# Thirteen whole quads of a graph kernel's key/value gather loaded row by row, in place of one tile of each of 42 quads

## The chip, the cores and the metric

The kernel runs on one core of one Trainium2 chip. The metric is device time in microseconds (us), from the launch of the one program to its end; lower is better. Each kernel is timed in several runs, and the median is shown with the lowest and the highest. The profile is one further execution, recorded by the hardware profiler; its span goes from the first to the last recorded instruction.

## The reference

A graph layer with attention-like edge weights, a residual and a layer norm. There are 6250 nodes with 128 features and 206250 edges, sorted by receiving node (`dst`); `src` are the senders.

```python
w_ij  = silu(edge_feats @ rad_W1 + rad_b1) @ rad_W2 + rad_b2
w_ij += silu(chi_scalar @ sph_W1 + sph_b1) @ sph_W2 + sph_b2          # per edge, 128
q_i   = (node_feats @ Wq)[receivers]
k_j   = (node_feats @ Wk)[senders]
v_j   = (node_feats @ Wv)[senders]
alpha = (q_i * w_ij * k_j).sum(over the 16 of each of 8 heads) / sqrt(16) * cutoffs
out   = segment_sum(alpha * v_j, receivers) / 16
x     = layernorm(x + out)                                            # rows without scale or shift
```

## The kernel before

**Tiling.** Edges lie on the 128 partitions. A tile is 128 edges, a quad four tiles (`QT = 4`, 512 edges), a group four quads (`NQ = 4`). There are 403 quads (`QUADS`) in 101 groups (`NG`). A prologue computes K and V of all nodes (`k_and_v`), writes them to a table in DRAM, `kv_tab`, with 1 KB a node (`ROW_BYTES`), and prepares index tables. For the first ten quads (`XQ`) K and V are computed from gathered rows of x; for the 393 others they are gathered from `kv_tab`.

**The gather.** `gathers(q)` lets POOL (GpSimd) issue one indirect DMA a tile (L132, through the helper `gather`): it fetches the 1 KB rows of 128 senders into one quarter of a `kv` buffer. There are `RING = 16` such buffers, and the gather of the quad 14 positions ahead (`AHEAD`) is issued in each slot of the main loop, with a wait on the matmuls of an earlier quad.

**The main loop** (L746 to L808) has one slot a quad, in the order 0, 2, 1, 3 within a group (the list `order`). In a slot, each engine's queue gets its work in the order of the code:

- PE: sums of messages of the group before (L616), the two first layers of the quad two ahead (`first_layers`, L518, into two `ph` buffers), q at the edges of the next quad (L527), the second layers of the next quad (`weigh`, L560 and L565). One slot in a group also has the sum over a whole group (L657, L659).
- ACT (ScalarE): the two silus of the quad two ahead (L548; the first waits for the q matmuls of L527), between them two row loads (`next_rows(2)`), then a copy out of PSUM, and at the end of the slot up to four more row loads (`rows_at_end`). Once in 16 slots `statistics` normalizes four groups: a table load for the square root, L682, four L696, and a table load back before the next silu.
- DVE (VectorE): `multiply` (L577, q times K; it reads `kv`), `scores` (L585, L587, L591), `messages` (L604, alpha times V), and one-hot matrices (`hotT` L264 from `relb`, `hot` L269).
- SP: the DMA queue for x rows (L283), edge features (L224), `relb` (L235), the result's rows (`write_rows`, L708), and row loads (L191).

**Rows loaded singly.** 42 quads of the 403 (`ROW_TILES`, positions `row_at`) have only three of their four tiles gathered by POOL. The fourth is loaded by 128 single DMAs of 1 KB, whose addresses come from registers: `load_rows(i)`, called at the end of slot i, has SP load 32 addresses into registers (L186, `ROW_UNIT`) and issue 32 DMAs (L191), two and a half times a tile (80 rows); and ACT loads 24 addresses (`ROW_UNIT_ACT`) and issues 24 DMAs, twice a tile (48 rows, `ROW_ACT`), spread over slots by `next_rows` and `rows_at_end`. The rows of a tile go out over the 8 or 9 slots between two such quads and are complete 8 slots (`ROW_LEAD`) before use. They land in a `wide` buffer, of which there are three, and `multiply` waits for their count on a semaphore (`row_sems`). As the tiles of such a quad lie in two buffers (`kv_parts`), L577 and L604 run twice there, over 384 and 128 columns.

**The result's rows.** `normalize` puts four results into the list `written`; `write_rows`, one call a slot, pops one and queues its DMA on SP. The call stands ahead of `statistics` in the slot, so the first row of a batch is queued in the slot after its normalization.

Of the kernel before, what the change touches and what calls it, by code (L numbers as in the profile page):

```python
# [65 lines left out]
def gnn_kernel(ctx, tc, x, src, dst, weight, edges, rad_W1, rad_b1, rad_W2, rad_b2,  # L66
# [77 lines left out]
    row_sems = [tc.alloc_semaphore(f"rows_{n}") for n in range(ROW_SEMS)]  # L144
    row_count = [0] * ROW_SEMS

    def next_rows(n):
# [16 lines left out]
    def gathers(q, marks=()):  # L164

        kv = quad_of("kv", RING, 2 * D)
        for t in range(QT - 1 if q in row_quads else QT):
            o = gather(kv[:, t, :], kv_tab, src_i[:, q * QT + t:q * QT + t + 1])
            if marks:
                tc.add_manual_dep(o.ins, marks[t].ins.name, WAIT, reason="no gather ahead of TensorE")  # L170
        kv_of[q] = kv

    def load_rows(i):

        k = next((k for k in range(ROW_TILES) if i <= row_at[k] - ROW_LEAD), None)
        start = len(order) if k is None else (row_at[k - 1] if k else ROW_FIRST) - ROW_LEAD + 1
        if i < start:
            return rows_at_end() if k is None else None
        q = order[row_at[k]]
        n = P - ROW_ACT  # L180
        slots, units = row_at[k] - ROW_LEAD + 1 - start, math.ceil(n / ROW_UNIT)
        a, b = ((j * units + slots - 1) // slots for j in (i - start, i - start + 1))
        table = kv_tab.bitcast(U8).rearrange("(o n) b -> o (n b)", o=1)

        def registers(e, m, engine):
            return nc.values_load_multi_w_load_instructions(  # L186
                at_i[k:k + 1, e:e + m], engines=(engine,), min_val=0,
                max_val=(N - 1) * ROW_BYTES, skip_runtime_bounds_check_because="senders are nodes")[1]

        def one_row(engine, p, r):  # L190
            return engine.dma_start(row_of[q][p:p + 1, 0, :].bitcast(U8), table[:, ds(r, ROW_BYTES)])  # L191

        def rows_of_act(first, m):
            rows = registers(first, m, ACT)
            for p in range(m):
                yield lambda p=p: signalled(one_row(nc.scalar, first + p, rows[p]))

        def signalled(o):
            tc.no_tile_sem_insts.add(o.ins.name)
            tc.add_to_no_dep_group(f"rows_{q}", o.ins)  # L200
            o.then_inc(row_sems[k % ROW_SEMS], 16)
            row_count[k % ROW_SEMS] += 16
            row_done[q] = row_sems[k % ROW_SEMS], row_count[k % ROW_SEMS]
# [12 lines left out]
    def kv_parts(q, t):  # L216

        if q not in row_quads:
            return [(t, kv_of[q][:, t, :])]
        return [(slice(0, QT - 1), kv_of[q][:, :QT - 1, :]), (slice(QT - 1, QT), row_of[q])]  # L220

# [85 lines left out]
    with tc.tile_pool(name="nodes", bufs=1) as nodes, \  # L307
# [79 lines left out]
        def row_bytes():  # L387
            for k, i in enumerate(row_at):
                c = order[i] * QT + QT - 1
                nc.vector.tensor_scalar(rows_f[:, k:k + 1], src_i[:, c:c + 1],  # L390
                                        float(ROW_BYTES), None, op0=OP.mult)
# [120 lines left out]
    with tc.tile_pool(name="ps", bufs=1, space=PSUM) as pp:  # L512
# [57 lines left out]
        def multiply(q, mark=None, t=slice(0, QT)):  # L570
            if t.start == 0:
                kq_of[q] = quad_of("kq", 3)
            if t.start == 0 and q in row_done:
                o = nc.vector.wait_ge(*row_done[q])
                tc.declare_fence(o.ins, group=f"rows_{q}")
            for u, kv in kv_parts(q, t):
                o = nc.vector.tensor_tensor(kq_of[q][:, u, :], pq_of[q][:, u, :], kv[:, :, :D],  # L577
                                            op=OP.mult)
                if mark is not None:
                    after(o, mark)  # L580

# [16 lines left out]
        def messages(q, alpha, t=slice(0, QT), marks=()):  # L598

            if t.start == 0:  # L600
                msg_of[q] = quad_of("msg", XQ)
            for u, kv in kv_parts(q, t):
                n = u.stop - u.start
                o = nc.vector.tensor_tensor(  # L604
                    msg_of[q][:, u, :].rearrange("p t (h e) -> p t h e", e=HD),
                    kv[:, :, D:].rearrange("p t (h e) -> p t h e", e=HD),
                    alpha[:, u.start - t.start:u.stop - t.start, :, None].to_broadcast(
                        [P, n, HEADS, HD]), op=OP.mult)
                behind(o, marks, 3)

        def sum_quads(g, t, j=None):
# [6 lines left out]
            return o  # L618

        def wide_one_hots(q):  # L620

# [3 lines left out]
            nc.vector.tensor_scalar(d, d, gb[:, q // NQ:q // NQ + 1], None, op0=OP.subtract)  # L625
            hot_of[q, "wide"] = quad_of("wide", 3, P)
            nc.vector.tensor_tensor(hot_of[q, "wide"], d[:, :, None].to_broadcast([P, QT, P]),
# [116 lines left out]
        marks = weigh(order[0])  # L744
        mark = marks[-1]
        for g in range(NG - 1):  # L746
            for slot, j in enumerate((0, 2, 1, 3)):
# [34 lines left out]
                if slot == 1:  # L782
# [82 lines left out]
    def general_group(g):  # L865
        with tc.tile_pool(name="lg", bufs=1) as lg, tc.tile_pool(name="lb", bufs=1) as lb, \
# [12 lines left out]
            for j in range(NQ):  # L879
                kv = lb.tile([P, QT, 2 * D], F32, name="kv_l")  # L880
                qe = lb.tile([P, QT, D], F32, name="qe_l")
                xe = lb.tile([P, QT, D], F32, name="xe_l")
# [8 lines left out]
                for t in range(QT):  # L891
                    nc.tensor.matmul(pq[:, t, :], xe[:, t, :], wq, start=True, stop=True)
                nc.vector.tensor_copy(qe, pq)
                r0, c0 = 2 * R * (j // 2), EQ * (j % 2)
# [120 lines left out]
```

## Time and profile before

| | |
|---|---|
| median of 3 runs | 1985.04 us (1985.03 to 1985.54) |
| the profiled execution, its own time | 1985.41 us |
| its span | 1983.3 us |
| mean granted TensorE clock | 0.916 |
| ACT busy / share of the span | 752.2 us / 38% |
| DVE busy / share | 1471.1 us / 74% |
| POOL busy / share | 1488.6 us / 75% |

The busy time of an engine counts its computing instructions (and on POOL the indirect DMAs); loads of registers, semaphore waits and the issue of a DMA on SP or ACT don't count, and are listed under "SPq" and "ACTq". In a list of groups, each row has the line of the code, the engine, the operation, what it writes and reads, how often, the busy time in us and the mean in ns, and then the idle time of the engine just ahead of these instructions with what ended it. In the list of waits, a row is the engine and line that waited, what released it, the total in us, the number of times and the longest. A timeline row is start, length, engine, line and operation, and in brackets the engine's idle time before it with its releaser.

### The profile page before, as it was taken

The numbers are of one execution on the slowest core, as the hardware profiler recorded it, in microseconds if no ns is written. First come the engines' busy times: TensorE is split into PE (matmuls) and PEld (weight loads), VectorE is DVE, ScalarE is ACT, GpSimd is POOL, SyncE is SP. The second block draws the span as 40 slices with busy tenths as digits, with TensorE's granted clock in tenths as the row PEclk, the third lists the DMA queues.
The fourth block names the chain that finished last, engine by engine and source line by source line (L and its number), as shares of the span: only waits on it lengthen the run. The fifth ranks groups of instructions, "written<-read, shape, count | busy, mean of one in ns | idle before, by whom it ended". The sixth has DMA issues, their size and how long they took to land.

```text
span 1983.3 us, 55295 instructions
## 1 busy us (share of the span) xinstructions
PE 1782.5 (90%) x16014; PEld 1505.7 (76%) x16014; DVE 1471.1 (74%) x3123; ACT 752.2 (38%) x1437; POOL 1488.6 (75%) x1580
## 2 busy tenths in 40 slices
PE   9899999978997988998898888899989988898897
PEld 7788788767876877876787777777767777777786
DVE  6687777768876877776777777767767767777777
ACT  3244344333343343342343333333433433433334
POOL 7777777777777777777777777777777777777775
PEclk9899899978998998998999889989989999898988
DMA  8545545455455555454554555545545455445543
GB/s 316 160 141 156 157 145 156 142 157 156 143 157 154 146 156 154 144 160 139 159 158 140 159 142 155 158 143 154 154 145 158 144 152 159 142 142 158 157 140 90
DMA packets 150194, 304.77 MB, mean 154 GB/s; under 512 B 38732, under 2 KB 83900, under 8 KB 149884
## 3 DMA queue, kind: packets, MB, share of 16 engines
q0 software_dynamic: 74720, 203.26, 36.7%
q1 hardware_dynamic: 69632, 95.45, 14.8%
q10 hardware_dynamic: 5532, 2.47, 0.5%
q8 instruction: 128, 2.10, 0.4%
q14 instruction: 182, 1.49, 0.3%
HBM read 287.58 MB, written 13.46 MB: 152 GB/s over the span
## 4 chain that ended last, share of the span: by engine, by line
PE 56%; DMA 17%; DVE 11%; issue 6%; POOL 3%; ACTq 2%; SPq 2%; ACT 2%; DVEq 0%; POOLq 0%
PE pw L565 28%; DMA kv<-kv_tab,src_i 14%; PE pq L527 10%; PE ph L518 7%; PE po L616 4%; DVE kq L577 4%; DMA relb<-rel_lin 3%; PE pw L560 3%; ACTq L191 2%; POOL msg L132 2%; DVE side L587 2%; DVE kq L585 2%; SPq L191 1%; PE pq L657 1%; POOL kv L132 1%
## 5 line engine op out<-in xcount | busy, mean ns | idle before, releaser
L132 POOL DMA_INDIRECT kv<-kv_tab,src_i x1530 | 1447.9, 946 | 466.6 <-PE pw L565 174.2
L548 ACT ACTIVATE act<-ph,b 128x512 f32<-128x512 f32 x806 | 546.5, 687 | 1091.0 <-PE pq L527 1003.5
L565 PEld LDWEIGHTS pw<-w,act 128*128 128x128 f32 x6448 | 822.8, 207 | 105.6 <-issue 94.7
L565 PE MATMUL pw<-w,act 128*128 128x128 f32 x6448 | 902.7, 298 | 0.0
L527 PE MATMUL pq<-q,hotT 32*128 32x128 f32 x3224 | 502.9, 299 | 50.8 <-DVE hotT L264 40.4
L518 PE MATMUL ph<-feats,w 32*128 32x512 f32 x1612 | 501.2, 680 | 31.5 <-ACT act L548 30.6
L527 PEld LDWEIGHTS pq<-q,hotT 32*128 32x128 f32 x3224 | 422.8, 200 | 75.9 <-issue 55.4
L577 DVE TENSOR_TENSOR kq<-pq,kv 128x512 f32<-128x512 f32 (+1 forms) x403 | 271.8, 674 | 243.8 <-PE pq L527 121.2
L587 DVE TENSOR_REDUCE side<-kq 128x32 f32<-128x512 f32 x403 | 280.1, 695 | 43.2 <-DVE kq L585 1.4
L604 DVE TENSOR_TENSOR msg<-kv,side 128x512 f32<-128x512 f32 (+1 forms) x404 | 271.9, 673 | 42.7 <-DVE side L591 1.2
L585 DVE TENSOR_TENSOR kq<-pw,kq 128x512 f32<-128x512 f32 x403 | 274.7, 682 | 0.0
L518 PEld LDWEIGHTS ph<-feats,w 32*128 32x128 f32 x1612 | 137.9, 193 | 113.7 <-issue 58.2
L560 PE MATMUL pw<-brow,onesb 3*128 3x512 bf16 x403 | 161.9, 402 | 9.4 <-DVE kq L585 9.3
L616 PE MATMUL po<-msg,hot 128*32 128x128 f32 x3200 | 154.6, 290 | 0.0
L264 DVE TENSOR_TENSOR hotT<-relb,side 128x512 f32<-128x512 bf16 x101 | 69.0, 683 | 97.5 <-DMA relb<-rel_lin 97.4
L657 PE MATMUL pq<-part,to 128*128 128x128 f32 x200 | 45.9, 313 | 82.6 <-DVE kq L577 58.0
L591 DVE TENSOR_TENSOR side<-side,scale 128x32 f32<-128x32 f32 x400 | 80.0, 200 | 42.3 <-DVE side L587 0.5
L657 PEld LDWEIGHTS pq<-part,to 128*128 128x128 f32 x200 | 31.3, 197 | 93.0 <-issue 54.0
L616 PEld LDWEIGHTS po<-msg,hot 128*32 128x32 f32 x3200 | 71.3, 111 | 38.3 <-issue 4.8
L269 DVE TENSOR_TENSOR hot<-rel,side 128x512 f32<-128x512 f32 x100 | 66.1, 661 | 0.0
L258 PE MATMUL pq<-wq,xT 128*128 128x128 f32 x200 | 42.9, 299 | 11.2 <-DVE kq L577 11.1
L132 POOL DMA_INDIRECT msg<-in_x,src_x x40 | 38.9, 972 | 13.3 <-issue 11.6
(117 smaller groups left out, 855.6 us busy)
## 6 DMA issues: line engine op xcount, KB each, us to landing
wide<-kv_tab SPq DMA_DIRECT2D x3360, 1.0 KB
feats<-in_edges SPq DMA_DIRECT2D x101, 512.0 KB
wide<-kv_tab ACTq DMA_DIRECT2D x2016, 1.0 KB
kv<-kv_tab,src_i POOLq DMA_INDIRECT x1530
relb<-rel_lin SPq DMA_DIRECT2D x101, 128.0 KB
x<-in_x SPq DMA_DIRECT2D x101, 64.0 KB
out<-y SPq DMA_DIRECT2D x101, 64.0 KB
kv_tab<-kv SPq DMA_DIRECT2D x12, 512.0 KB
```

What stands on the lines that cost most here:

```text
L132: return nc.gpsimd.indirect_dma_start(out=o, out_offset=None, in_=table, in_offset=bass.IndirectOffsetOnAxis(ap=index, axis=0))
L518: return nc.tensor.matmul(act_of[q, i], w1[r0:r0 + R, :], feats_of[g][r0:r0 + R, c0:c0 + EQ], start=True, stop=True)
L527: o = nc.tensor.matmul(pq_of[q][:, t, :], hotT_of[g][b, t * P:(t + 1) * P], q_of[g][b, :], start=True, stop=True)
L548: o = nc.scalar.activation(act, act_of[q, i], AF.Silu, bias=b1[:, i:i + 1])
L560: nc.tensor.matmul(pw, onesb, brow.rearrange("p t d -> p (t d)"), start=True, stop=False)
L565: o = nc.tensor.matmul(pw[:, t, :], act_of[q, i][:, t * P:(t + 1) * P], w2[:, i, :], start=False, stop=(t == QT - 1 and i == 1))
L577: o = nc.vector.tensor_tensor(kq_of[q][:, u, :], pq_of[q][:, u, :], kv[:, :, :D], op=OP.mult)
L585: nc.vector.tensor_tensor(m, pw_of[q][:, t, :], m, op=OP.mult)
L587: o = nc.vector.tensor_reduce(alpha, m.rearrange("p t (h e) -> p t h e", e=HD), AX.X, OP.add)
L604: o = nc.vector.tensor_tensor(msg_of[q][:, u, :].rearrange("p t (h e) -> p t h e", e=HD), kv[:, :, D:].rearrange("p t (h e) -> p t h e", e ...
L616: o = nc.tensor.matmul(po_of[g][j * W:(j + 1) * W, :], hot_of[g][:, j * QT + t, :], msg_of[g * NQ + j][:, t, :], start=(t == 0), stop=(t = ...
L657: nc.tensor.matmul(ph[:, :D], to[:n, 0, :], part[:n, :], start=True, stop=(g == 0))
```

## The change

13 quads (`ROW_QUADS`) get all their four tiles by single rows, 52 tiles in all, and POOL gathers nothing for them (`gathers` returns at once, and such a quad takes no `kv` buffer). Of the 128 rows of a tile SP loads 64 and ACT 64, each in two units of 32 registers. `row_slots` gives each of the 52 tiles 7 or 8 slots of its own; within these ACT's rows go out against a goal for each slot, with no upper limit per slot. The four tiles of a quad lie in one new `rows` buffer (two of them, 4 KB a partition each; the three `wide` buffers of 2 KB go, and the three wide one-hots of the end are put into `rows` buffers), so `multiply` and `messages` run once over 512 columns for every quad. `write_rows` is called with 0 in a slot unless rows had been left in `written` at the end of the slot's writing before, so a batch's first row is queued two slots after its normalization; from group NG - 2 on it is called with 1 as before. In the branch for general inputs, which isn't run here, one buffer is shared.

```diff
-ROW_TILES = 42
+ROW_QUADS = 13
+ROW_TILES = ROW_QUADS * QT
-ROW_ACT = 48
-ROW_UNIT_ACT = 24
-ROW_SLOT_ACT = 6
+ROW_ACT = 64
+ROW_UNIT_ACT = 32
...
-    row_at = [ROW_FIRST + (n + 1) * (ROW_LAST - ROW_FIRST) // ROW_TILES for n in range(ROW_TILES)]
+    row_at = [ROW_FIRST + (n + 1) * (ROW_LAST - ROW_FIRST) // ROW_QUADS for n in range(ROW_QUADS)]
+    row_slots = []
+    for n, last in enumerate(row_at):
+        first = (row_at[n - 1] if n else ROW_FIRST) - ROW_LEAD + 1
+        row_slots += [first + t * (last - ROW_LEAD + 1 - first) // QT for t in range(QT)]
+    row_slots.append(row_at[-1] - ROW_LEAD + 1)
...
     def next_rows(n):
         for _ in range(min(n, len(act_now))):
             act_now.pop(0)()
-
-    def rows_at_end():
-        n = ROW_SLOT_ACT - 2
-        m = min(n, len(act_now))
-        next_rows(m)
-        if not act_now and act_rows:
-            f, e, r = act_rows.pop(0)
-            act_now.extend(f(e, r))
-            next_rows(n - m - 1)
+            act_sent[0] += 1
+
+    def rows_at_end(goal):
+        while act_sent[0] < goal:
+            if not act_now:
+                f, e, r = act_rows.pop(0)
+                act_now.extend(f(e, r))
+            next_rows(min(len(act_now), goal - act_sent[0]))
...
     def gathers(q, marks=()):
+        if q in row_quads:
+            return
         kv = quad_of("kv", RING, 2 * D)
-        for t in range(QT - 1 if q in row_quads else QT):
+        for t in range(QT):
...
-        q = order[row_at[k]]
-        n = P - ROW_ACT
-        slots, units = row_at[k] - ROW_LEAD + 1 - start, math.ceil(n / ROW_UNIT)
+        start, slots = row_slots[k], row_slots[k + 1] - row_slots[k]
+        at, t = divmod(k, QT)
+        q, n = order[row_at[at]], P - ROW_ACT
+        units = math.ceil(n / ROW_UNIT)
...
-        if i == start:
-            row_of[q] = quad_of("wide", 3, P)[:, :2, :].rearrange("p t d -> p (t d)")[:, None, :]
+        if i == start and t == 0:
+            row_of[q] = quad_of("rows", 2, 2 * D)
...
-        rows_at_end()
+        rows_at_end(k * ROW_ACT + ROW_ACT * (i - start + 1) // slots)
...
-            for u, kv in kv_parts(q, t):
-                o = nc.vector.tensor_tensor(kq_of[q][:, u, :], pq_of[q][:, u, :], kv[:, :, :D],
-                                            op=OP.mult)
+            kv = (row_of if q in row_quads else kv_of)[q]
+            o = nc.vector.tensor_tensor(kq_of[q][:, t, :], pq_of[q][:, t, :], kv[:, t, :D], op=OP.mult)
...
+        made_before = 0
         for g in range(NG - 1):
...
-                write_rows()
+                write_rows(1 if made_before or g >= NG - 2 else 0)
+                made_before = len(written)
```

`messages` is changed as `multiply` is, and `row_bytes`, in the prologue, makes the 52 columns of byte addresses by 13 instructions of four columns, where it made 42 columns by 42 instructions.

More of the change, by code (lines that the diff above doesn't have):

```diff
@@ L173, in load_rows @@
     def load_rows(i):
[L175 to L178, printed above, removed]
-        q = order[row_at[k]]
-        n = P - ROW_ACT
-        slots, units = row_at[k] - ROW_LEAD + 1 - start, math.ceil(n / ROW_UNIT)
+        k = next((k for k in range(ROW_TILES) if i < row_slots[k + 1]), None)
+        if k is None or i < row_slots[k]:
+            return
+        start, slots = row_slots[k], row_slots[k + 1] - row_slots[k]
+        at, t = divmod(k, QT)
+        q, n = order[row_at[at]], P - ROW_ACT
+        units = math.ceil(n / ROW_UNIT)
         a, b = ((j * units + slots - 1) // slots for j in (i - start, i - start + 1))
@@ L387, in row_bytes @@
         def row_bytes():
-            for k, i in enumerate(row_at):
-                c = order[i] * QT + QT - 1
-                nc.vector.tensor_scalar(rows_f[:, k:k + 1], src_i[:, c:c + 1],
+            for n, i in enumerate(row_at):
+                c = order[i] * QT
+                nc.vector.tensor_scalar(rows_f[:, n * QT:(n + 1) * QT], src_i[:, c:c + QT],
                                         float(ROW_BYTES), None, op0=OP.mult)
@@ L575, in multiply @@
                 tc.declare_fence(o.ins, group=f"rows_{q}")
[L576 to L580 removed]
+            kv = (row_of if q in row_quads else kv_of)[q]
+            o = nc.vector.tensor_tensor(kq_of[q][:, t, :], pq_of[q][:, t, :], kv[:, t, :D], op=OP.mult)
+            if mark is not None:
+                after(o, mark)
         def scores(q, t=slice(0, QT), marks=(), weighted=True):
@@ L601, in messages @@
                 msg_of[q] = quad_of("msg", XQ)
[L602 to L609, printed above, removed]
+            kv = (row_of if q in row_quads else kv_of)[q]
+            o = nc.vector.tensor_tensor(
+                msg_of[q][:, t, :].rearrange("p t (h e) -> p t h e", e=HD),
+                kv[:, t, D:].rearrange("p t (h e) -> p t h e", e=HD),
+                alpha[:, :, :, None].to_broadcast([P, t.stop - t.start, HEADS, HD]), op=OP.mult)
+            behind(o, marks, 3)
         def sum_quads(g, t, j=None):
@@ L625, in wide_one_hots @@
             nc.vector.tensor_scalar(d, d, gb[:, q // NQ:q // NQ + 1], None, op0=OP.subtract)
-            hot_of[q, "wide"] = quad_of("wide", 3, P)
+            if q != order[-2]:
+                wides.append(quad_of("rows", 2, 2 * D))
+            hot_of[q, "wide"] = wides[-1][:, :, P:] if q == order[-2] else wides[-1][:, :, :P]
             nc.vector.tensor_tensor(hot_of[q, "wide"], d[:, :, None].to_broadcast([P, QT, P]),
```

16 lines of the change are left out of this document (7 added, 9 removed).

## The prediction, made before the changed kernel ran

> **What bounds the kernel now.** I read the page first: the busy list, the chain that ended last, and the costliest group.
>
> ```profile
> PE 1782.5 (90%) x16014; PEld 1505.7 (76%) x16014; DVE 1471.1 (74%) x3123; ACT 752.2 (38%) x1437; POOL 1488.6 (75%) x1580
> ...
> PE 56%; DMA 17%; DVE 11%; issue 6%; POOL 3%; ACTq 2%; SPq 2%; ACT 2%; DVEq 0%; POOLq 0%
> ...
> L132 POOL DMA_INDIRECT kv<-kv_tab,src_i x1530 | 1447.9, 946 | 466.6 <-PE pw L565 174.2
> ```
>
> PE looks like the bound, at 90% and 56% of the chain, and POOL, at 75%, does not. But POOL's row deserves a second look: 1447.9 busy and 466.6 idle ahead of its 1530 gathers make 1914.5 us, 1.251 us a gather. The list of POOL's waits and its first and last gathers in the timeline say what the idle time is.
>
> ```profile
> POOL kv L132 <- PE pw L565: 174.2, 571, 0.3
> POOL kv L132 <- issue: 172.3, 565, 0.3
> POOL kv L132 <- DMA kv<-kv_tab,src_i: 46.0, 151, 0.3
> ```
>
> ```profile
> 54.12 1.03 POOL L132 DMA_INDIRECT kv<-kv_tab,src_i  x1 [0.30 <-DVE b_all L379]
> ...
> 1967.39 0.94 POOL L132 DMA_INDIRECT kv<-kv_tab,src_i  x1 [0.30 <-issue]
> ```
>
> No gap is longer than 0.3 us, whatever is named as its releaser. From 54.12 to 1967.39 the 1530 gathers start every (1967.39 - 54.12) / 1529 = 1.251 us: POOL is full from end to end, and the 0.3 us belong to each gather. Whether the others wait for it, VectorE's waits for gathered rows tell: first those between 520 and 860 us, then those between 900 and 1960 us, and last its waits for `relb` over the whole span.
>
> ```profile
> DVE kq L577 <- DMA kv<-kv_tab,src_i: 1.1, 1, 1.1
> ...
> DVE kq L577 <- DMA kv<-kv_tab,src_i: 83.9, 55, 3.7
> ...
> DVE hotT L264 <- DMA relb<-rel_lin: 97.4, 26, 12.3
> ```
>
> So there are two phases. In the first PE and VectorE, which start behind the gathers, catch up and hardly wait for rows. In the second they have caught up, wait for gathers 55 times, and the pace is POOL's. The end is POOL's last gather plus 1983.3 - 1967.4 = 15.9 us of tail, and the compute side has about 84 us in hand.
>
> **The change, part by part.** *Gathers.* 393 quads of four tiles less 42 leave 1530; less 52 they leave 1520. Ten gathers at 1.251 us are 12.5 us off POOL's stretch. Leaving out four in a row instead of one lets POOL run one quad ahead; the ring holds 14, so nothing else changes, and the last such position is 392 in both kernels, ahead of the tail. All four gathers of a row quad are spared there at once, so the 12.5 us are complete eleven quads before the end.
>
> *Row loads on ACT and SP.* Their prices, from the rows of the two lines (min/median/max in ns):
>
> ```profile
> L191 SPq DMA_DIRECT2D wide<-kv_tab x3360: 224/228/436, 125.0 to 1883.9; - x198
> L191 ACTq MOVE wide<-kv_tab x2016: 29/29/29, 128.9 to 1888.8; - x184
> L191 ACTq DMA_DIRECT2D wide<-kv_tab x2016: 227/228/706, 129.0 to 1888.8; - x184
> ...
> L186 SPq TENSOR_LOAD <-at_i x126: 979/1924/2497, 122.9 to 1877.2; - x126
> L186 ACTq TENSOR_LOAD <-at_i x84: 1662/1780/2070, 127.0 to 1871.1; - x84
> ```
>
> SP issues 3328 rows instead of 3360 and loads registers 104 times (32 each) instead of 126 (84 of 32, 42 of 16, the short ones near the minimum of 0.98): some 32 x 0.32 = 10 us and 42 x 0.98 - 20 x 1.92 = 3 us less over the run. SP's queue is as full as before.
>
> ACT issues 3328 rows instead of 2016, and loads 32 registers 104 times instead of 24 registers 84 times. That is 3328 / 372 = 8.9 rows a slot against 5.4. What covers them is the wait of the first silu for PE. A slot of ACT now, and PE's next first layer:
>
> ```profile
> 1003.22 0.69 ACT L548 ACTIVATE act<-ph,b 128x512 f32<-128x512 f32 x1 [2.93 <-PE pw L565]
> 1003.30 0.55 ACTq L191 DMA_DIRECT2D wide<-kv_tab  x2
> 1003.95 0.69 ACT L548 ACTIVATE act<-ph,b 128x512 f32<-128x512 f32 x1
> 1004.05 0.68 ACTq L191 DMA_DIRECT2D wide<-kv_tab  x2
> 1004.53 0.27 ACT L661 ACTIVATE tot<-pq 128x128 f32<-128x128 f32 x1
> 1004.82 0.58 ACTq L191 DMA_DIRECT2D wide<-kv_tab  x2
> 1006.60 0.69 ACT L548 ACTIVATE act<-ph,b 128x512 f32<-128x512 f32 x1 [1.80 <-PE pq L527]
> ```
>
> ```profile
> 1005.30 0.70 PE L518 MATMUL ph<-feats,w 32*128 32x512 f32 x2
> ```
>
> Two rows take 0.55 us, the second 0.32 after the first, and they lie beside the activations. Six rows end 2.18 us after the first silu's start; the next silu comes 3.38 after it. Nine rows end at 3.15: still covered, in a slot as short as this. With a register load it is another matter:
>
> ```profile
> 1031.17 0.69 ACT L548 ACTIVATE act<-ph,b 128x512 f32<-128x512 f32 x1 [2.03 <-PE pq L527]
> ...
> 1031.99 0.58 ACTq L191 DMA_DIRECT2D wide<-kv_tab  x2
> 1032.48 0.27 ACT L652 ACTIVATE part<-po 128x128 f32<-128x128 f32 x1
> 1034.57 0.47 ACTq L191 DMA_DIRECT2D wide<-kv_tab  x1
> 1035.14 0.69 ACT L548 ACTIVATE act<-ph,b 128x512 f32<-128x512 f32 x1 [2.40 <-PE pw L565]
> ```
>
> Between 1032.57 and 1034.57 ACT's queue loads 24 registers, and five rows end 3.87 us after the silu. With 32 registers (1.92 by SP's row, 1780 / 24 x 32 = 2.37 by ACT's) and nine rows (four more, 1.28) that is 5.3 to 5.7 us. The next silu is then about 2.2 late behind a slot of 3.4 us, 0.8 behind an average one (1983 / 403 = 4.9). PE forgives part: the second silu ended at 1004.64, 0.66 before PE began the next first layer, whose first half needs the first silu alone, 0.7 earlier; some 1.35 in all. So a load slot costs PE between nothing (average slot) and about 0.9 us (short slot); 104 of them cost 0 to 94 us. I take half, 47, as the recorded slots are of both kinds. What is queued behind the late silu on ACT is the copy out of PSUM and the slot's rows; who waits is PE.
>
> The slots with a table change have no such cover:
>
> ```profile
> 1015.49 1.25 ACT L696 ACTIVATE y<-y,shift,rs 128x128 f32<-128x128 f32 x3
> 1017.37 0.79 ACTq L191 DMA_DIRECT2D wide<-kv_tab  x2
> 1018.24 1.28 ACT L548 ACT_TABLE_LOAD   x1 [1.51 <-issue]
> ...
> L548 ACT ACT_TABLE_LOAD x25 | 32.1, 1283 | 7.9 <-issue 7.4
> ```
>
> There rows go out beside the four normalizations (three take 1.25 us, four some 1.7). Four rows (1.28) fit, seven (2.24) stick out by 0.5: 13 us in 25 slots. Where a register load falls into such a slot (104 / 372 or 28% of them, 7) another 2.4 us stand free: 17. Before, these slots lost 7.4. Together 23 us more, 0 as the other end.
>
> *Sum on ACT:* 47 + 23 = 70 us of PE's time, 0 to 117. Part of it is no loss: `relb` comes when SP's queue has got to it, and a PE that arrives later waits less of those 97.4 us. I take a third as covered so and keep 47. Against it stand the 83.9 us in hand, less the 12.5 that POOL gives up: 71. So 47 stays hidden, but not by much.
>
> *Result rows.* SP's waits:
>
> ```profile
> SPq L708 <- DMA out<-y: 122.7, 50, 5.5
> SPq L708 <- ACT y L696: 68.0, 9, 29.8
> SPq L224 <- PE pq L527: 41.5, 12, 11.0
> ```
>
> Queued a slot later, a row finds its normalization done; that spares SP at most 68.0 - 29.8 = 38 us (the longest is at the end, which is unchanged). The waits of one write for the other stay. What is behind them on SP are rows, `feats` and `relb`, so `relb` comes a little sooner. At POOL's pace this pays nothing; I count 0, and 38 as the other end, within PE's room.
>
> *VectorE.* In 42 quads two instructions become one, twice:
>
> ```profile
> L577 DVE TENSOR_TENSOR kq<-pq,kv 128x512 f32<-128x512 f32 x361 | 248.5, 688 | 218.7 <-PE pq L527 102.4 <-DMA kv<-kv_tab,src_i 80.1 <-PE pw L565 26.3
> ...
> L577 DVE TENSOR_TENSOR kq<-pq,kv 128x384 f32<-128x384 f32 x42 | 23.3, 555 | 25.1 <-PE pq L527 18.8 <-DMA kv<-kv_tab,src_i 5.7 <-PE pw L565 0.3
> ...
> L577 DVE TENSOR_TENSOR kq<-pq,wide 128x128 f32<-128x128 f32 x42 | 11.8, 282 | 0.0
> ```
>
> (555 + 282 - 688) x 84 = 12.5 us of VectorE, off the path while it waits for rows: 0. The `wait_ge` in `multiply` is met, as a quad's rows are due eight slots (39 us) before; the address instructions of the prologue lie beside gathers that already run. SP's and ACT's row bytes are the same bytes that POOL's gathers no longer fetch.
>
> **Sum.** The profiled execution's own time is 1985.41, 2.1 over its span and 0.37 over the median. 1985.41 - 12.5 = 1972.9; against the median, 1985.04 - 12.5 = **1972.5 us**.
>
> **The rivals.**
>
> *ACT becomes the bound (slower).* Place: the slots in which ACT loads 32 registers ahead of its rows. If all lose what the short slot loses and nothing is covered by `relb`, PE loses 117 us, 46 more than its 71: 1972.5 + 46 = 2018. It decides from 71 us on, a mean of (71 - 23) / 104 = 0.46 us a load slot, just what I took for the average. For it: in the quoted load slot ACT is already the last to be ready. Against it: today's loads cost PE little, and in the second phase PE waits for rows anyway.
>
> *PE is the bound already (no change).* Then ten gathers fewer only lengthen POOL's lead: 1985. For it: PE 90% busy, 56% of the chain. Against it: 55 waits for rows in the second phase, and none of POOL for anything.
>
> *The descriptor hardware is shared (slower).* If every row that ACT issues held up SP for its 0.228 us, 1312 more would cost SP 299 us; its waits above sum to 232, so at least 67 would come out at `relb`: about 2040. Against it: SP's median row, 228 ns, is 4 ns above its minimum, though ACT issues rows all the while. [...]
>
> **How the numbers follow.** Forecast 0.62, ACT's bound 0.22, no change 0.09, shared hardware 0.07. The forecast's own range is 1969 (a few us from SP and VectorE in the tail) to 1978 (a part of ACT's delay comes through). The range of 1969 to 2016 takes in no change and most of what ACT's bound can give. A measurement of this kernel tells about 0.2% (4 us) from no change: faster 0.62, within 0.09, slower 0.29.
>
> **What would show it.** Right: 1520 gathers, still with no gap over 0.3 us, the last starting at about 1955; fewer than 84 us of waits for rows in the second phase, but still some near the end. Wrong: gaps on POOL or no waits for rows near the end (PE has fallen behind), with first layers (L518) waiting for `act`, or silus whose idle time ends at "issue" (ACT's rows); SP's median row well over 228 ns (shared hardware); a `wait_ge` of microseconds in `multiply` (rows late).

## The result, and the profile after

| | before | after |
|---|---|---|
| median on the same chip, 5 runs each | 1985.03 us (1984.36 to 1985.54) | 1995.71 us (1991.50 to 1999.19) |
| ratio | 1 | 1.0052, 95% [1.0035, 1.0069] |
| profiled execution, own time / span | 1985.41 / 1983.3 us | 1991.50 / 1989.6 us |
| mean granted TensorE clock | 0.916 | 0.925 |

The change makes the kernel 0.5% slower; the forecast was 0.6% faster. The profiled execution is the fastest of the five, so what follows accounts for its 6.3 us of longer span and not for the 10.7 us between the medians. In three of the six batches of runs the kernel before itself takes 2659 to 2667 us on the chip of that batch; every ratio is therefore against before on the same chip, and the two kinds of batch are kept apart.

The page of the changed kernel (busy list, chain, gathers and the table load):

```profile
PE 1803.3 (91%) x16014; PEld 1511.4 (76%) x16014; DVE 1463.9 (74%) x3010; ACT 748.0 (38%) x1437; POOL 1478.5 (74%) x1570
...
PE 55%; DMA 10%; ACTq 9%; DVE 8%; issue 8%; ACT 5%; POOL 2%; SPq 2%; DVEq 0%; POOLq 0%
...
L132 POOL DMA_INDIRECT kv<-kv_tab,src_i x1520 | 1437.8, 946 | 463.7 <-PE pw L566 166.9
...
L549 ACT ACT_TABLE_LOAD x25 | 32.1, 1283 | 37.4 <-issue 32.0
```

DMA's share of the chain fell from 17% to 10%, and ACT's queue rose from 2% to 9%. POOL's timeline at the end says what no longer bounds:

```profile
1954.33 0.94 POOL L132 DMA_INDIRECT kv<-kv_tab,src_i  x1 [0.30 <-issue]
1974.43 0.47 POOL L676 TENSOR_TENSOR y<-tot,x 128x128 f32<-128x128 f32 x1 [19.16 <-ACT tot L663]
```

POOL delivered: its last gather starts 1967.39 - 1954.33 = 13.06 us earlier than before. But from there to the end it is 1989.6 - 1954.3 = 35.3 us instead of 15.9, and POOL waits 19.16 us for the others. PE is behind, and the list of waits names two causes:

```profile
PEld ph L519 <- ACT act L549: 154.3, 201, 5.2
...
DVE hotT L265 <- DMA relb<-rel_lin: 127.8, 28, 9.9
PE ph L519 <- ACT act L549: 90.0, 76, 4.9
...
DVE kq L578 <- DMA kv<-kv_tab,src_i: 32.5, 27, 6.7
```

VectorE's waits for gathered rows fell from 85.9 to 32.5 us, 13.3 of them in two single waits of 6.6 and 6.7; its waits for `relb` rose from 97.4 to 127.8. (Those two follow two of the longest waits of PE's first layers for a silu, 4.86 and 4.90 us, and VectorE starts within 0.1 us of the end of PE's q products, so they are hardly POOL's.) What this costs PE is best read from the groups of PE's matmuls (busy time, mean ns, then the idle time just ahead of them), first of before, then of after:

```profile
L527 PE MATMUL pq<-q,hotT 32*128 32x128 f32 x3224 | 502.9, 299 | 50.8 <-DVE hotT L264 40.4 <-DVE kq L577 10.4
L518 PE MATMUL ph<-feats,w 32*128 32x512 f32 x1612 | 501.2, 680 | 31.5 <-ACT act L548 30.6 <-ACT relT L441 0.7 <-issue 0.2
L560 PE MATMUL pw<-brow,onesb 3*128 3x512 bf16 x403 | 161.9, 402 | 9.4 <-DVE kq L585 9.3
...
L657 PE MATMUL pq<-part,to 128*128 128x128 f32 x200 | 45.9, 313 | 82.6 <-DVE kq L577 58.0 <-ACT y L696 24.6
L258 PE MATMUL pq<-wq,xT 128*128 128x128 f32 x198 | 42.3, 298 | 11.2 <-DVE kq L577 11.1
```

```profile
L519 PE MATMUL ph<-feats,w 32*128 32x512 f32 x1612 | 546.5, 664 | 91.6 <-ACT act L549 90.0 <-ACT relT L442 0.7 <-issue 0.6
L528 PE MATMUL pq<-q,hotT 32*128 32x128 f32 x3224 | 493.2, 295 | 65.6 <-DVE kq L578 65.6
...
L659 PE MATMUL pq<-part,to 128*128 128x128 f32 x200 | 41.3, 289 | 15.7 <-ACT y L698 9.6 <-DVE kq L578 5.8 <-issue 0.3
```

Busy and idle time of PE add up to the span, so the difference of the two kernels can be booked row by row. *First layers:* 501.2 + 31.5 = 532.7 became 546.5 + 91.6 = 638.1, **+105.4 us**. (The 45.3 us of it that count as busy are no work: one matmul got shorter, 680 to 664 ns, but they overlap less: 1612 x 680 ns are 1096 us in 501.2 of busy time before, 1612 x 664 ns are 1070 in 546.5 after. In the slot at 1516.86 of the timeline further down, PEld waits 0.43 us for the second silu ahead of the second pair, while matmuls of L519 still run; PEld's 154.3 us are therefore not added.) *q products* (L527, L528): 50.8 to 65.6, **+14.8**. *Waits elsewhere*, in which PE was ahead and waited for VectorE or a normalization (L657, L560, L258): 82.6 + 9.4 + 11.2 = 103.2 became 15.7, **-87.5**. *Busy time of all other matmuls:* 1782.5 - 501.2 = 1281.3 became 1803.3 - 546.5 = 1256.8, **-24.5**. Together +8.2 us; the span grew by 6.3. So PE lost 120 us at two places, and 112 could be covered. To profit from POOL's 12.5 us it would have had to cover all of it and 12.5 more.

The q products' row of after names L578, VectorE's multiplication, and not `relb`. But in the code the multiplication stands behind the one-hots, and the timeline has it so: in the longest of these waits it starts at 908.36, 1.33 us after the one-hot that had waited for `relb`. On SP's queue, VectorE and PE:

```profile
896.53 0.58 SPq L236 DMA_DIRECT2D relb<-rel_lin  x1
```

```profile
907.03 0.69 DVE L265 TENSOR_TENSOR hotT<-relb,side 128x512 f32<-128x512 bf16 x1 [9.94 <-DMA relb<-rel_lin]
```

```profile
909.18 2.04 PE L528 MATMUL pq<-q,hotT 32*128 32x128 f32 x8 [6.70 <-DVE kq L578]
```

By the timelines of the two engines, 64.2 of the 65.6 us after, and 41.7 of the 50.8 before, came behind such a wait for `relb`.

### The profile page after: what moved, and what is told of

Same layout as the page of the kernel before. It is cut to its first block, busy times and chain, and to the rows that moved or that the text cites. A ratio compares the mean times of both kernels' runs of the same rounds, so it can differ in the third digit from the quotient of the medians.

```text
span 1989.6 us, 57573 instructions
## 1 busy us (share of the span) xinstructions
PE 1803.3 (91%) x16014; PEld 1511.4 (76%) x16014; DVE 1463.9 (74%) x3010; ACT 748.0 (38%) x1437; POOL 1478.5 (74%) x1570
## 4 chain that ended last, share of the span: by engine, by line
PE 55%; DMA 10%; ACTq 9%; DVE 8%; issue 8%; ACT 5%; POOL 2%; SPq 2%; DVEq 0%; POOLq 0%
PE pw L566 26%; PE pq L528 10%; PE ph L519 10%; ACTq L198 7%; DMA kv<-kv_tab,src_i 6%; PE po L614 4%; ACT act L549 3%; DMA relb<-rel_lin 3%; DVE kq L578 2%; PE pw L561 2%; ACTq L193 2%; POOL msg L132 2%; DVE side L587 1%; SPq L198 1%; DVE kq L585 1%
## 5 line engine op out<-in xcount | busy, mean ns | idle before, releaser
L519 PE MATMUL ph<-feats,w 32*128 32x512 f32 x1612 | 546.5, 664 | 91.6 <-ACT act L549 90.0
L528 PE MATMUL pq<-q,hotT 32*128 32x128 f32 x3224 | 493.2, 295 | 65.6 <-DVE kq L578 65.6
L528 PEld LDWEIGHTS pq<-q,hotT 32*128 32x128 f32 x3224 | 413.9, 197 | 84.8 <-issue 82.1
L578 DVE TENSOR_TENSOR kq<-pq,kv 128x512 f32<-128x512 f32 x390 | 268.3, 688 | 215.4 <-PE pq L528 178.3
L519 PEld LDWEIGHTS ph<-feats,w 32*128 32x128 f32 x1612 | 158.6, 190 | 211.0 <-ACT act L549 154.3
L587 DVE TENSOR_REDUCE side<-kq 128x32 f32<-128x512 f32 x403 | 280.1, 695 | 41.7 <-PE pw L566 0.2
L603 DVE TENSOR_TENSOR msg<-kv,side 128x512 f32<-128x512 f32 x391 | 268.5, 687 | 42.8 <-DVE side L591 2.6
L265 DVE TENSOR_TENSOR hotT<-relb,side 128x512 f32<-128x512 bf16 x101 | 69.0, 683 | 127.9 <-DMA relb<-rel_lin 127.8
L561 PE MATMUL pw<-brow,onesb 3*128 3x512 bf16 x403 | 160.6, 399 | 0.0
L614 PE MATMUL po<-msg,hot 128*32 128x128 f32 x3200 | 149.8, 283 | 0.0
L659 PE MATMUL pq<-part,to 128*128 128x128 f32 x200 | 41.3, 289 | 15.7 <-ACT y L698 9.6
L698 ACT ACTIVATE y<-y,shift,rs 128x128 f32<-128x128 f32 x100 | 41.4, 482 | 11.7 <-DVE shift L694 11.7
```

The source lines that it names most:

```text
L519: return nc.tensor.matmul(act_of[q, i], w1[r0:r0 + R, :], feats_of[g][r0:r0 + R, c0:c0 + EQ], start=True, stop=True)
L528: o = nc.tensor.matmul(pq_of[q][:, t, :], hotT_of[g][b, t * P:(t + 1) * P], q_of[g][b, :], start=True, stop=True)
L561: nc.tensor.matmul(pw, onesb, brow.rearrange("p t d -> p (t d)"), start=True, stop=False)
L578: o = nc.vector.tensor_tensor(kq_of[q][:, t, :], pq_of[q][:, t, :], kv[:, t, :D], op=OP.mult)
L587: o = nc.vector.tensor_reduce(alpha, m.rearrange("p t (h e) -> p t h e", e=HD), AX.X, OP.add)
L603: o = nc.vector.tensor_tensor(msg_of[q][:, t, :].rearrange("p t (h e) -> p t h e", e=HD), kv[:, t, D:].rearrange("p t (h e) -> p t h e", e ...
```

## The experiments

Two theories stood against each other. *ACT's queue:* its loads of 32 registers and its denser rows make the silus late. *SP's queue:* rows, result writes and loads follow one another there, and `relb` comes later. The table has PE's account, made as above, for seven kernels that ran where before takes 1985 to 1989 us (us, from one profile each; the changed kernel itself was run in the first batch alone):

| kernel | first layers | q products' waits | waits elsewhere | other busy | span | ratio |
|---|---|---|---|---|---|---|
| before | 532.7 | 50.8 | 103.2 | 1281.3 | 1983.3 | 1 |
| after | 638.1 | 65.6 | 15.7 | 1256.8 | 1989.6 | 1.0052 |
| ACT's rows in a block (e5) | 524.2 | 36.3 | 115.1 | 1286.7 | 1975.8 | 0.9939 |
| SP's rows in a block (e6) | 631.0 | 13.1 | 55.5 | 1260.5 | 1975.5 | 0.9944 |
| ACT's registers loaded once (e7) | 541.8 | 104.8 | 45.4 | 1281.2 | 1986.0 | 0.9995 |
| result rows as before (e8) | 641.6 | 58.0 | 21.4 | 1260.0 | 1992.4 | 1.0039 |
| ACT's units of 16 (e12) | 620.2 | 88.5 | 19.6 | 1245.3 | 1985.8 | 1.0023 |

**ACT's rows in one block.** One DMA of 64 neighbouring rows takes the place of 64 of the senders' rows (other values, the same bytes), with no register loads on ACT.

```diff
-            act_rows.extend((rows_of_act, e, min(ROW_UNIT_ACT, P - e)) for e in range(n, P, ROW_UNIT_ACT))
-        rows_at_end(k * ROW_ACT + ROW_ACT * (i - start + 1) // slots)
+            signalled(nc.scalar.dma_start(row_of[q][n:, t, :], kv_tab[n:P, :]))
```

> ACT's 64 rows of a tile come by one DMA of 64 neighbouring rows of the table (so these rows are not the senders'), SP's 64 singly as in the changed kernel. Theory A (ACT's row loads and register loads delay the silus, and PE with them): PE catches up with the gathers again, POOL sets the end, about 1973 us, with VectorE's waits for gathered rows back at some 80 us. Theory S (SP's queue brings relb too late): no change, 1990 to 2000. Theory P (PE is the bound by itself): no change.

> The first four ran on a chip on which the kernel before itself took 2659 us and POOL had gaps, so they don't answer for the kernel at 1985. The same kernel again: ACT's 64 rows of a tile by one DMA of 64 neighbouring rows, SP's 64 singly. Where the kernel before takes 1985: theory A (ACT's row and register loads make the silus late) says 1973, POOL setting the end, and waits of PE's first layers for act back at about 70 us in all (244 in the changed kernel); theory S (SP brings relb late) and theory P (PE by itself) say 1990 to 2000.

Where before takes 1988.66 us it took 1976.65, ratio 0.9939 [0.9923, 0.9956]. The waits:

```profile
DVE kq L577 <- DMA kv<-kv_tab,src_i: 153.4, 94, 4.6
...
PEld ph L518 <- ACT act L548: 32.9, 35, 2.9
...
PE ph L518 <- ACT act L548: 22.3, 23, 2.7
...
DVE hotT L264 <- DMA relb<-rel_lin: 20.2, 5, 6.7
```

The first layers lose nothing (524.2 us against 532.7 before), and the waits for gathered rows are back: POOL's bound with ten gathers fewer, 12.0 us under before. But `relb`'s waits also fell from 127.8 to 20.2 us, although SP's work is unchanged, so this run alone doesn't choose between the two theories. On the chip where before takes 2658.87 us the ratio was 0.9934 [0.9913, 0.9955].

**SP's rows in one block**, the same for SP's 64 rows:

```diff
-        for e in range(a * ROW_UNIT, min(min(b, units) * ROW_UNIT, n), ROW_UNIT):
-            m = min(ROW_UNIT, n - e)
-            rows = registers(e, m, SP)
-            for p in range(m):
-                signalled(one_row(nc.sync, e + p, rows[p]))
+            signalled(nc.sync.dma_start(row_of[q][:n, t, :], kv_tab[:n, :]))
```

> SP's 64 rows of a tile come by one DMA of 64 neighbouring rows of the table (not the senders'), ACT's 64 singly as in the changed kernel. Theory A: relb waits vanish, but the silus stay late: 1985 or more. Theory S: PE catches up, about 1973 us. Theory P: 1990 to 2000.

> The same kernel again: SP's 64 rows of a tile by one DMA of 64 neighbouring rows, ACT's 64 singly. Where the kernel before takes 1985: theory A says the waits for relb (127.8 us) vanish but PE's waits for act stay near 244, and the end lies between 1975 and 1995, as a part of the lag was relb's; theory S says 1973; theory P 1990 to 2000.

1977.47 us, ratio 0.9944 [0.9928, 0.9961].

```profile
PEld ph L515 <- ACT act L545: 141.4, 166, 5.3
DVE kq L574 <- DMA kv<-kv_tab,src_i: 107.7, 75, 6.7
...
PE ph L515 <- ACT act L545: 87.7, 68, 5.0
```

Here ACT's queue is as it is after the change, and PE loses as much at its first layers (631.0 against 638.1), yet the full gain is there, and no wait for `relb` is left. ACT's delay alone stays hidden; what decides is added by SP. As the block takes far more off SP than the change had added, the run shows that SP's lateness is needed for the loss, and not how much of it is new. On the chip with 2658.87 us it was otherwise: 1.0072 [1.0050, 1.0094].

**ACT's registers loaded once.** ACT keeps its first 32 addresses and fetches the same rows for every tile (other values); its rows stay single.

```diff
-            rows = registers(first, m, ACT)
+            if not act_kept:
+                act_kept.append(registers(first, m, ACT))
+            rows = act_kept[0]
```

> ACT loads its 32 row addresses once and issues every later row from these registers (its rows are not the senders'); the number of rows a slot is unchanged, 103 register loads of 2.2 us are gone. Theory A, by its load slots: no slot of ACT is longer than 3.3 us any more, POOL sets the end, about 1973. Theory A, by the rows themselves (9 a slot): stays above 1985. Theory S: 1990 to 2000.

> The same kernel again: ACT loads 32 addresses once and issues all its rows from them. Where the kernel before takes 1985: theory A by the load slots says 1973, with no slot of ACT's queue beyond 3.4 us but those with a table change; theory A by the rows (9 a slot) says above 1985; theory S 1990 to 2000.

1987.14 us against 1988.66, ratio 0.9995 [0.9984, 1.0006].

```profile
DVE hotT L268 <- DMA relb<-rel_lin: 207.1, 39, 15.8
...
PEld ph L522 <- ACT act L552: 60.3, 45, 3.0
...
PE ph L522 <- ACT act L552: 47.4, 25, 2.7
```

96 of the first layers' 105 us are gone (541.8 against 638.1): they come with the register loads, not with the rows. But the time only returns to that of before, because the waits for `relb` grew from 127.8 to 207.1 us: with the silus on time, PE gets to the next place earlier and waits there. So SP's lateness alone eats the gain of the gathers. And beside e5, which has neither ACT's loads nor its single rows, it shows where that lateness is from: with the loads away and the rows left it stays, with the rows away too it goes. On the other chip: 1.0205 [1.0182, 1.0228].

**Result rows written as before**, the rest as after:

```diff
-                write_rows(1 if made_before or g >= NG - 2 else 0)
+                write_rows()
```

> The changed kernel with write_rows() called as before, one row in each slot from the slot after the normalization on. Where the changed kernel takes 1996: if the later sending helps SP (relb sooner), this is slower, 1998 to 2010; if it costs, since 187.5 us of SP's waits for one row's write by the next stand against 122.7 before, it is faster, 1985 to 1993; if it lies off the path, 1990 to 2000.

1995.55 us, 1.0039 [1.0025, 1.0053], an interval that overlaps that of the change (1.0035 to 1.0069): this part of the change moves no time that can be told. SP's waits of one result write for the one before are as long as with the change:

```profile
SPq L710 <- DMA out<-y: 178.2, 55, 6.0
```

**ACT's units of 16 registers** instead of 32: as many registers, in 208 shorter loads.

```diff
-ROW_UNIT_ACT = 32
+ROW_UNIT_ACT = 16
```

> ACT loads its addresses in units of 16 instead of 32, 208 loads in place of 104. If what counts is ACT's queue time beyond a short slot of PE, slots of 5.7 us in two of seven become slots of 4.8 in four of seven, and the sum is about the same: 1988 to 2000. If what counts is the single long slot (more than PE forgives), the time falls to 1973 to 1982.

> ACT loads its addresses in units of 16 instead of 32, on a chip where the kernel before takes some 1985. If what counts is ACT's queue time beyond a short slot of PE, the time stays at 1.002 to 1.007 of the kernel before; if what counts is the single long slot, it falls to 0.994 to 0.999.

1988.12 us, 1.0023 [1.0011, 1.0034]; on the other chip 1.0238 [1.0212, 1.0263]. The first layers lose 18 us less (620.2 against 638.1), and the waits for `relb` grow from 127.8 to 145.6 us, as with e7 in a smaller measure. The ratio lies where the queue time of ACT was expected to put it (1.002 to 1.007), and far from what the single long slot would have given (0.994 to 0.999).

**`relb` one group earlier**, in a third buffer: on the changed kernel (e9), on the kernel before as a control (e10), and with 15 whole quads instead of 13 (e11). To make room for it, one buffer is shared in the branch for general inputs, which isn't run here.

```diff
-        relb_of[g] = gp.tile([P, EQ], BF16, name="relb")
+        relb_of[g] = gp.tile([P, EQ], BF16, name="relb", bufs=3)
...
+        load_rel(2)
...
-                    if g + 2 < NG:
-                        load_rel(g + 2)
+                    if g + 3 < NG:
+                        load_rel(g + 3)
```

> The changed kernel with relb loaded one group (four slots) earlier, into a third buffer. Taking all of ACT's rows away, or all of SP's, each brought the end to POOL's bound, so neither ACT's delay nor relb's alone seems to hold PE behind. Theory AS (the lag is the sum of the two, and either one fits beside POOL): waits for relb near 0, waits of first layers for act as in the changed kernel (244), and 0.993 to 0.996 of the kernel before. Theory A (ACT alone decides): 1.000 to 1.005, as now.

> The kernel before with the same earlier relb. It is at POOL's bound already: its waits for relb (97.4 us) vanish, its waits for gathered rows grow by about as much, and the time stays within 0.2%. If relb had a share in the time before, it is faster by more than that.

> As the changed kernel with relb a group earlier, and 15 quads (60 tiles) in place of 13: 1488 gathers, 32 fewer, at most 40 us more off POOL's stretch; ACT and SP issue 10.3 rows a slot. Theory AS: with relb out of the way ACT has some 20 us left, so PE falls behind again; between 0.985 and 1.000 of the kernel before. If ACT alone decides: above 1.005.

The control's time didn't change, 1985.59 us, 1.0002 [0.9993, 1.0011], though its waits for `relb` fell from 97.4 to 4.0 us; those for gathered rows rose from 85.9 to 135.7. On the changed kernel the median is **1978.90 us against 1984.71, 0.9978 [0.9965, 0.9991]**, the one version of this study that computes everything and is faster than before. It is not steady: 12 runs spread from 1974.58 to 1991.70, and the profiled one is the slowest of them. The ratio lies between what the two theories had expected. The profile shows what became of the waits (list of waits):

```profile
PEld ph L519 <- ACT act L549: 140.8, 173, 5.2
PE ph L519 <- ACT act L549: 84.5, 71, 5.0
...
DVE hotT L265 <- DMA relb<-rel_lin: 51.0, 11, 7.1
...
PE pq L250 <- DMA x<-in_x: 44.5, 10, 7.5
...
PE ph L519 <- DMA feats<-in_edges: 33.0, 7, 6.4
```

`relb`'s waits fell from 127.8 to 51.0, and the next things in SP's queue are late in its place: x rows, 0.3 in the changed kernel and 44.5 here, and edge features, not on its list and 33.0 here. In this execution it is the queue that is late, not this one load; what the faster ones waited for isn't on record.

With 15 quads (60 tiles, 10.3 rows a slot on each queue) I expected 0.985 to 1.000, or above 1.005 if ACT alone decided, and was far off: 2194.62 us, 1.1049 [1.1033, 1.1065].

```profile
PEld ph L519 <- ACT act L549: 206.2, 205, 5.7
...
PE ph L519 <- ACT act L549: 137.1, 96, 5.5
...
PE pq L250 <- DMA x<-in_x: 84.1, 17, 11.9
...
DVE hotT L265 <- DMA relb<-rel_lin: 82.4, 21, 10.1
...
PE ph L519 <- DMA feats<-in_edges: 53.3, 15, 8.4
```

What comes through SP is now waited for 84.1 + 82.4 + 53.3 = 220 us, and ACT's silus cost PE more too, 137.1 against 84.5 in e9; the mean granted clock was 0.878. Why two more quads cost as much as 200 us wasn't isolated.

**Who should fetch the rows, and who should write the results.** Two batches fell on chips where before takes 2667.43 and 2665.53 us. There the 128 rows of a tile were split 80 to 48 (e13, e17: ACT 80; e14: ACT 48, all else as after), and the result's rows were thinned out (e15: as after, without the writes of three of four result rows up to the last eight groups) or given to ACT (e16, e18: e9 with the write on ACT's queue).

```diff
-ROW_ACT = 64
+ROW_ACT = 80
```

```diff
-                nc.sync.dma_start(rows_from(out, r_of.pop(g)), y.bitcast(U8))
+                if g % LB == 0 or g >= NG - 2 * LB:
+                    nc.sync.dma_start(rows_from(out, r_of.pop(g)), y.bitcast(U8))
```

```diff
-                nc.sync.dma_start(rows_from(out, r_of.pop(g)), y.bitcast(U8))
+                at = nc.values_load(gb_i[:1, g:g + 1], engines=(ACT,), ...)
+                nc.scalar.dma_start(rows_from(out, at), y.bitcast(U8))
```

> The changed kernel with 80 rows of a tile by ACT and 48 by SP. Theory S (SP's queue is full, and feats, x and relb come at its pace): 832 rows and half of its second register loads fewer are some 320 us off SP, PE catches up, 0.993 to 0.997 of the kernel before. Theory A (ACT decides): 11.2 rows a slot, 1.01 or more. Theory AS (the sum): between the two.

> The changed kernel with 48 rows by ACT and 80 by SP, in 52 tiles. Theory S: 320 us more on a queue that is full, 1.08 to 1.16 of the kernel before. Theory A: ACT has 6.7 rows a slot, PE catches up, 0.993 to 0.997.

> The changed kernel without the writes of three in four of the result's rows (up to the last eight groups): 69 writes fewer on SP and most of the 187.5 us that a write waits for the one before. Theory S: 0.993 to 0.998 of the kernel before. Theory A: 1.002 to 1.007, as the changed kernel.

> relb a group earlier (as e9), and the result's rows written by ACT's queue, which loads their address itself. Theory S: SP is relieved by some 200 us, 0.993 to 0.996 of the kernel before, without the scatter of e9. Theory A: ACT carries 100 register loads and writes more, 1.00 or above.

> The same kernel as e13: 80 rows of a tile by ACT, 48 by SP. Where the kernel before takes 1985: theory S (SP's full queue paces PE) says 0.993 to 0.998, waits for relb below 40 us; theory A (ACT's late silus pace PE) 1.01 or more, PE's waits for act well over the 244 us of the changed kernel; theory AS, the sum of both, 0.997 to 1.01.

> The same kernel as e16: relb a group earlier, the result's rows written by ACT's queue. Where the kernel before takes 1985: theory S and theory AS say 0.993 to 0.996, POOL setting the end and less scatter than e9; theory A 1.00 or above.

e13 1.0296 [1.0240, 1.0352] and e17 1.0323 [1.0289, 1.0357]; e14 1.1011 [1.0948, 1.1074]; e15 1.0193 [1.0140, 1.0246]; e16 1.0208 [1.0156, 1.0261] and e18 1.0239 [1.0206, 1.0273]. The changed kernel itself wasn't run on such a chip, so neither the splits nor the writes can be compared with it there, and these runs decide between no theories. One row of e14 is worth having:

```profile
DVE hotT L265 <- DMA relb<-rel_lin: 395.8, 47, 18.5
```

With 80 rows of a tile on SP, `relb` is waited for 395.8 us; on chips of this kind it was 11.0 us with 64 rows (e4, ACT's units of 16), and with 48 (e13, e17) no such wait is on the list. So there SP's queue holds 64 rows a tile, and not 80; the questions of the best split and of the best queue for the results stay open for a chip where before takes 1985 us.

## Why the prediction was wrong

**POOL: right.** 1520 gathers at 1.251 us without a longer gap, the last starting at 1954.33 where about 1955 was forecast; e5 and e6 show the 12.5 us arriving at the end (-12.0 and -11.2 us).

**SP "as full as before", cost 0: the step that failed and turned the sign.** The prediction counted SP's own work; of SP's waits it said that "the waits of one write for the other stay", and they didn't. SP's waits after the change, then in e5 and in e6:

```profile
SPq L710 <- DMA out<-y: 187.5, 56, 10.1
SPq L710 <- ACT y L698: 48.5, 5, 25.7
```

```profile
SPq L709 <- DMA out<-y: 92.4, 42, 5.6
```

```profile
SPq L706 <- DMA out<-y: 111.8, 31, 5.4
```

Writing a slot later spared 68.0 - 48.5 = 19.5 us, within the 38 that were given, but the waits of one result write for the one before grew from 122.7 to 187.5. The later writing isn't the cause, as e8 has 178.2 without it. A single wait is longer the more rows ACT issues singly: 92.4 / 42 = 2.2 us with none (e5), 122.7 / 50 = 2.5 with 2016 (before), 187.5 / 56 = 3.3 with 3328 (after), and 111.8 / 31 = 3.6 with 3328 beside an SP that issues no single rows (e6). `relb` lands later too: by the timelines, where VectorE waits for it, it starts on average 5.0 us after the end of SP's issue before (26 waits, at most 5.7), and 6.3 us after (28 waits, at most 9.9). That is an estimated 28 x 1.3 = 36 us, about as much as the waits for `relb` rose. Instead of "a little sooner", `relb` comes later. e6, which relieves SP and nothing else, brings 11.2 of the 12.5 us forecast; e7, which relieves ACT's loads and nothing of SP, brings none. The step that failed is thus shown; that ACT's single rows delay the landing of SP's transfers fits all the runs that were made where before takes 1985 to 1989 us, but no run took the result writes off SP there, and how much the later landing and the 45 us net of SP's waits each do wasn't separated.

**"A third as covered" by `relb`: wrong in sign, for the same reason.** A later PE was to wait less there. As what SP brings came later too, the q products wait 14.8 us more, although PE arrives later.

**ACT: the mechanism right, the term too small.** The changed kernel's timeline, ACT and then PE:

```profile
1510.50 0.69 ACT L549 ACTIVATE act<-ph,b 128x512 f32<-128x512 f32 x1 [3.57 <-PE pq L528]
...
1511.96 4.06 ACTq L198 DMA_DIRECT2D rows<-kv_tab  x5
1516.12 0.69 ACT L549 ACTIVATE act<-ph,b 128x512 f32<-128x512 f32 x1 [4.05 <-PE pw L566]
```

```profile
1512.81 0.70 PE L519 MATMUL ph<-feats,w 32*128 32x512 f32 x2
...
1513.82 0.38 PE L561 MATMUL pw<-brow,onesb 3*128 3x512 bf16 x1
...
1516.86 1.41 PE L519 MATMUL ph<-feats,w 32*128 32x512 f32 x3 [0.47 <-ACT act L549]
...
1518.15 0.39 PE L561 MATMUL pw<-brow,onesb 3*128 3x512 bf16 x1
```

The rows end at 1511.96 + 4.06 = 1516.02, 5.5 us after the silu (5.3 to 5.7 forecast). PE then waits 0.47, and from its first layer to L561 it takes 1.29 instead of 1.01, as the second silu is late too: 0.75 us, within the 0 to 0.9 that was given. Of the 105.4 us, the slots with a table change have 56.2 - 30.6 = 25.6 (the waits right behind a table load, 22 in each timeline; 23 was forecast). The other 79.8 us are 0.77 for each of 104 load slots. "I take half, 47" was the error: by the timeline, in 81 of the 104 the first layers of the slot behind the load take over 1.5 us, with their waits, where 1.13 is usual. The sum is 105 instead of 70, with 117 as the upper end.

**The room of 71 us: too small, and not one sum.** Counted by VectorE's waits for rows, it was 83.9 - 12.5. PE's own account gave 87.5 us of waits and 24.5 of shorter matmuls, against 105.4 + 14.8 = 120 lost. That the other matmuls got shorter was not in the forecast, and was luck. The sum alone doesn't decide either. e7 loses 541.8 + 104.8 - 532.7 - 50.8 = 63 us at the two places and e6 631.0 + 13.1 - 532.7 - 50.8 = 61, and e7 is 10 us longer. It has 20.7 us more in the other matmuls, and its waits fall elsewhere. VectorE's waits for `relb` behind 900 us, where the prediction let PE go at POOL's pace, are, before, after and in e7 (e6 has none):

```profile
DVE hotT L264 <- DMA relb<-rel_lin: 28.9, 7, 7.6
```

```profile
DVE hotT L265 <- DMA relb<-rel_lin: 86.0, 18, 9.9
```

```profile
DVE hotT L268 <- DMA relb<-rel_lin: 135.8, 24, 15.8
```

Before the change 68.5 of the 97.4 us lay ahead of 900 us. So the total, which rose by a third, hides that the waits of the second stretch tripled. Which of the two differences makes e7's 10 us wasn't tried.

**The rivals.** "ACT becomes the bound" named the place rightly, and its 117 us were nearer than my 70. It gave 2018 because it set them against a room of 71; ACT's delay alone stays hidden (e6). "PE is the bound already" is refuted by e5 and e6. "The descriptor hardware is shared" fails in the form given: SP's median row is 228 ns in both kernels, with 1312 more rows on ACT.

```profile
L198 SPq DMA_DIRECT2D rows<-kv_tab x3328: 224/228/435, 120.0 to 1897.5; - x196
L198 ACTq DMA_DIRECT2D rows<-kv_tab x3328: 227/228/813, 124.5 to 1904.7; - x196
```

That a row of ACT holds up SP for the whole 0.228 us at which this rival was priced shows in neither median; a shorter hold-up these rows don't decide, and what hardware the two queues share no run shows. SP pays in waits for landings (187.5 us for the result writes, against 122.7 before), not in issue.

**VectorE, `wait_ge`, prologue: right at 0.** VectorE's busy time fell by 7.2 us and paid nothing; no wait for single rows is on the list of waits.

## What to carry to other kernels

Work taken off a full engine pays only if the engines that take it over have room in the same slots (here 12.5 us came off POOL, PE lost 120 us at two places, and 112 could be covered): book it on the queue of the engine that waits (here PE, busy plus idle by line, which must add up to the span), and not by the idle share of the one that issues. A queue can get slower although its own work doesn't grow: its waits for landings have to be counted too, and here SP's waits for the result writes grew from 122.7 to 187.5 us, with 32 rows fewer on SP and 1312 more on ACT. Of two delays at once, remove each alone, and in two ways: here taking ACT's rows away also relieved SP's queue, and only the run with ACT's loads alone taken away showed that ACT's delay was not what decided (e7, 0.9995). Where loads stand late in one full queue, ordering one of them earlier can move the wait to the next of them: in e9 the waits for `relb` fell from 127.8 to 51.0 us, and those for x rows rose from 0.3 to 44.5. It can still be worth something (0.9978, against 1.0052).

## What the runs showed of the hardware that was not expected

- Before takes 1985 to 1989 us in three batches and 2659 to 2667 in the three others, the five of which the chip is on record each on another chip. In e1 (the same kernel as e5), run on one of the latter chips, POOL is not the bound; it waits for PE up to 20.0 us:

```profile
POOL kv L132 <- PE pw L565: 467.6, 257, 20.0
```

  The mean granted clock was 0.817 in e1 and 0.921 in e5. What makes the difference, and whether it is the chip, wasn't found.
- The mean granted clock also moves with the kernel: 0.916 before, 0.925 after, 0.934 in e6, 0.908 in e7. Why it moves wasn't tried. PE's busy time outside the first layers moves too, by as much as many terms of my sum (1281.3 before, 1256.8 after), but not by this clock alone: it is 1286.7 in e5 at 0.921 and 1245.3 in e12 at 0.922.
- A load of 32 registers took 2.21 us on ACT and 2.09 on SP (medians), the two ends of the forecast being 1.92 and 2.37.
